# Layer 3 in runs of 3, 8, 7 and 4 row tiles, with the last normalisation folded into weights

## The chip, the core and the metric

The kernel runs on one core of one Trainium2 chip. A core has five engines that run beside each other and meet only at semaphores: TensorE (matrix products, into PSUM), VectorE and ScalarE (element by element), GpSimd (the same, more slowly, and not on PSUM) and SyncE (which issues transfers). The metric is device time in microseconds, the median of several executions. Every engine executes its own instructions strictly in the order in which they were issued; an instruction that waits holds up all that are queued behind it on its engine.

## The reference, cut to what matters

Four graph layers follow one another, each on the normalised output of the one before, with 2708 nodes and 128 features. The change touches only the end of layer 3, an attention layer with two heads:

```python
def _L3_gnn_ref(x, adj, ff0_w, ff1_w, attn_w, g1, b1, g2, b2):   # x is h = relu(layernorm(xs))
    x_norm = _ln(x, g1, b1)
    mask = (adj > 0) | jnp.eye(n, dtype=bool)
    h_next = jnp.zeros((n, co), x.dtype)
    for i in range(2):
        h = x_norm @ ff0_w[i].T
        s_src = h @ attn_w[i, :c]
        s_dst = h @ attn_w[i, c:]
        e = jnp.where(mask, leaky_relu(s_src[:, None] + s_dst[None, :]), NEG)
        att = softmax(e, axis=1) @ h + x
        att = _ln(att, g2, b2)                       # (att - mean) / sqrt(var + eps) * g2 + b2
        h_next = h_next + elu(att @ ff1_w[i].T) / 2
    return h_next
...
h = jnp.maximum(_layernorm(x, axis=-1), 0.0)
x = x + _L3_gnn_ref(h, adj, ...)
```

## The kernel before, in words

The 2708 rows form 22 tiles of 128 rows; the last tile has 20. All of layer 3's inputs stay on the chip: `xs` (the rows so far), `h3` (their normalised, rectified form), `mask` (the transposed adjacency as bytes), `row` and `lift` (factors of the attention weights by destination and by source), and `hv` (128 features and a column of weights for the softmax denominator, per head).

The attention product is done in *runs* of row tiles, `RUNS = ((0, 3), (3, 8), (11, 8), (19, 3))`, each pair being first tile and number of tiles. `products` (L943 to L967) walks through 44 units per run (22 source tiles, two heads). For each unit VectorE first makes the weights of the whole run with one instruction, `weigh` (L930), into a tile `wt`; three units later in the issue order TensorE multiplies each 128-column piece of `wt` with `hv` (L960) and accumulates in PSUM. One product of 128x128 with 129 columns appears as two matmul records and two weight loads in the profile. Three sums of 129 columns share a PSUM bank, so a run of 8 tiles (16 sums) takes six banks and a run of 3 takes two.

Where the run's columns aren't a multiple of 128, as in the last run (276 columns), `weigh` writes into one of five tiles `padded`, which GpSimd sets once (L1238), in turn. Otherwise it takes one of five rotating buffers `wt`.

When a run is done, `evacuate` (L991) copies its banks from PSUM to SBUF, on ScalarE and every third one on VectorE, and `close` (L1012) finishes two row tiles (four sums) at a time: division by the denominator and addition of `h3` (L1023), row statistics and their power -1/2 on GpSimd (`moments`, L118 to L121), a Newton step and the shift (`factors`, L127 to L131), scaling on ScalarE (L137), four transposes on TensorE (L1034), a ScalarE copy that applies `g2` and `b2` (L1037), the second product with `ff1T` (L1043), the ELU in three ScalarE instructions (L1051 to L1053) with sums on GpSimd (L1055 to L1057), and two VectorE instructions (L1060, L1061) before the store to `out` (L1066).

The order on each engine is written out by hand. `close` is a generator; its `yield` gives a distance in ticks of a clock that `products` advances by 0.29 per tile and unit (`spend`), and `close` itself by its own TensorE work. `close_run` (L1068) begins a new pair every `apart` ticks, 9 by default. So the closes of a run are spread between the units of the next run. The last run has no run behind it: its sums are read where they are (`in_place`, L975), its two closes begin 2 ticks apart, and nothing covers them.

A flag, counted on the way (`lost_rows`), is turned into a count on TensorE and VectorE at the very end (L1707, L1708) and read by the engines; with a count over zero the program would go on with `dense_layers`.

Of the kernel before, what the change touches and what calls it, by code (L numbers as in the profile page):

```python
# [20 lines left out]
F32 = mybir.dt.float32  # L21
BF16 = mybir.dt.bfloat16
AF = mybir.ActivationFunctionType
# [7 lines left out]
P = 128  # L31
# [20 lines left out]
def size(t):  # L52
    return min(P, N - t * P)
# [7 lines left out]
def listed_layers(ctx: ExitStack, tc: tile.TileContext, x, adj, w, out, flag):  # L61
# [827 lines left out]
    score = l3.tile([P, NT, 4], F32, name="score")  # L889
    nc.gpsimd.memset(score[:, NT - 1, :], 0.0)  # L890
    nc.gpsimd.memset(hv[:, NT - 1, :, :], 0.0)
    nc.gpsimd.memset(lift[:, NT - 1, :], 0.0)
    nc.gpsimd.memset(mask[:, NT - 1, :], 0)
    ident_8 = l3.tile([P, P], U8, name="ident_8")
    nc.vector.tensor_copy(ident_8, ident)
    PIECE = 5
    RUNS = ((0, 3), (3, 8), (11, 8), (19, 3))
    MOST = 8
    accs = ctx.enter_context(tc.tile_pool(name="l23p", bufs=1, space=PSUM))

# [4 lines left out]
    def follow(steps):  # L905
        following.append([steps, clock[0]])
# [62 lines left out]
    def banks_of(run, numbers):  # L969
# [1 line left out]
            accs.tile([P, CH], F32, tag=f"acc{b}", name="att")[:, 0 : 3 * (D + 1)].rearrange("p (s d) -> p s d", s=3)  # L971
            for b in numbers[0 : (2 * run[1] + 2) // 3]
        ]

    def in_place(run, banks):  # L975

        r0, rn = run
        sums = [banks[s // 3][:, s % 3, :] for s in range(2 * rn)]
        inv3 = out_pool.tile([P, 2 * MOST], F32, name="inv3")
        for k in range(2):  # L980
            for q0, q1 in ((0, rn - 1), (rn - 1, rn)):
                m, s = size(r0 + q1 - 1), k * rn
                if q1 > q0:
                    nc.vector.reciprocal(
                        inv3[0:m, s + q0 : s + q1], banks[s // 3][0:m, (s + q0) % 3 : (s + q1 - 1) % 3 + 1, D]
                    )
        return sums, inv3, False

    def evacuate(run, banks):

        r0, rn = run  # L991
        res = out_pool.tile([P, 2 * MOST, D + 1], F32, bufs=1, name="res")
        inv3 = out_pool.tile([P, 2 * MOST], F32, name="inv3")
        tails = (rn - 1, 2 * rn - 1) if size(r0 + rn - 1) < P else ()
        for s in tails:
            nc.gpsimd.memset(res[:, s, :], 1.0)
        s = 0
        while s < 2 * rn:
            k = min(3 - s % 3, 2 * rn - s)
            m = P  # L1000
            if s in tails:
                k, m = 1, TAIL
            elif s + k - 1 in tails:
                k -= 1
            copy = nc.vector.tensor_copy if s // 3 % 3 == 2 else nc.scalar.copy
            copy(res[0:m, s : s + k, :], banks[s // 3][0:m, s % 3 : s % 3 + k, :])
            s += k
        nc.vector.reciprocal(inv3[:, 0 : 2 * rn], res[:, 0 : 2 * rn, D])
        return [res[:, s, :] for s in range(2 * rn)], inv3, True

    def close(run, sums, first):

        res, inv3, whole = sums
        k0 = min(2, run[1] - first)
        t0 = run[0] + first
        n = 2 * k0
        att = out_pool.tile([P, 4, D], F32, name="att_s")
        for s in range(n):
            i = s % 2 * run[1] + first + s // 2
            m = P if whole else size(t0 + s // 2)  # L1020
            if m < P:
                nc.gpsimd.memset(att[:, s, :], 0.0)
            nc.vector.scalar_tensor_tensor(  # L1023
                att[0:m, s, :], res[i][0:m, 0:D], inv3[0:m, i : i + 1], h3[0:m, t0 + s // 2, :],
                op0=ALU.mult, op1=ALU.add,
            )
        rows = tiles_of(att, 0, n)
        mv = moments(rows, "n4")
        yield 4.5
        scale_rows(rows, rows, *factors(*mv), AF.Identity)  # L1030
        yield 4
        p = bank("p_aT")
        for s in range(n):
            nc.tensor.transpose(p[:, s * P : (s + 1) * P], att[:, s, :], ident)  # L1034
        spend(0.25 * n)
        zT = out_pool.tile([P, 4, P], F32, name="z4T")
        nc.scalar.activation(  # L1037
            zT[:, 0:n, :], p.rearrange("p (s i) -> p s i", s=4)[:, 0:n, :], AF.Identity, bias=shift2, scale=gain2
        )
        yield 1.5  # L1040
        p = bank("p_o")
        for s in range(n):
            nc.tensor.matmul(  # L1043
                p[:, s * D : (s + 1) * D], zT[:, s, :], ff1T[:, s % 2 * D : (s % 2 + 1) * D], start=True, stop=True
            )
        spend(0.33 * n)

        v = p.rearrange("p (q k d) -> p q k d", q=2, k=2)[:, 0:k0, :, :]
        el = out_pool.tile([P, 2, 2, D], F32, name="el")[:, 0:k0, :, :]
        po = out_pool.tile([P, 2, 2, D], F32, name="po")[:, 0:k0, :, :]  # L1050
        nc.scalar.activation(el, v, AF.Relu, scale=-1.0)  # L1051
# [5 lines left out]
        nc.gpsimd.tensor_tensor(less[:, 0:k0, :], less[:, 0:k0, :], po[:, :, 0, :], ALU.add)  # L1057
# [3 lines left out]
        nc.vector.scalar_tensor_tensor(  # L1061
            y[:, 0:k0, :], el[:, :, 0, :], 0.5, less[:, 0:k0, :], op0=ALU.mult, op1=ALU.add
        )
        for q in range(k0):
            m, i = size(t0 + q), (t0 + q) * P
            nc.sync.dma_start(out[i : i + m, :], y[0:m, q, :])  # L1066

    def close_run(run, sums, apart=9):  # L1068
# [164 lines left out]
    nc.vector.reduce_sum(over, wide, AX.XY)  # L1233
    nc.vector.tensor_tensor(flag, flag, over, ALU.add)

    for q in range(5):
        padded.append(out_pool.tile([P, RUNS[-1][1] * P], F32, tag=f"padded{q}", bufs=1, name=f"padded{q}"))
        nc.gpsimd.memset(padded[q], 0.0)  # L1238

    with tc.tile_pool(name="l3w", bufs=5) as wpool, tc.manual_schedule():  # L1240
        for run, numbers in zip(RUNS[1:], ((2, 3, 4, 5, 0, 1), (2, 3, 4, 5, 0, 1), (2, 3))):

            def work_off(last=last, banks=banks):
                follow(close_run(last, evacuate(last, banks)))

            banks = products(run, numbers, wpool, 3, work_off)
            last = run
        follow(close_run(last, in_place(last, banks), 2))
        while following:
            spend(1)  # L1250
            advance()


@with_exitstack
# [459 lines left out]
```

## Time and profile before

| what | us |
|---|---|
| median of 3 runs (lowest, highest) | 1063.11 (1061.25, 1065.79) |
| the profiled execution | 1066.37 |
| its span | 1064.6 |
| run (3,8): first product to the next run | 829.7 to 911.8 |
| run (11,8) | 911.8 to 1000.2 |
| run (19,3) | 1000.2 to 1041.8 |
| last product to the last VectorE instruction | 1041.8 to 1058.6 |
| from there to the end of the span | 6.0 |

Over the whole span TensorE is busy 929.8 us (87%), VectorE 826.0 (78%), ScalarE 515.7 (48%) and GpSimd 402.1 (38%). Such shares are means over stages with different limits, so they say little about an edit at the end of layer 3; for this the span is cut into stretches and the order of instructions is read there.

In the profile PE is TensorE, PEld its weight load, DVE VectorE, ACT ScalarE, POOL GpSimd and SP SyncE. A timeline row gives start, length, engine, line, operation, output and inputs, shapes, and how many like instructions were merged into it; in brackets stands how long the engine had been idle before and what ended that. In a table by stretch each engine has its busy time and, in brackets, its number of instructions; then follow the clock that was granted to TensorE as a share of full speed, and the share and rate of the transfers.

### The profile page before, as it was taken

Reading aid. Unit: us, or ns where it says so; the run is one execution under the profiler, and the core shown is the slowest. Engines: PE = TensorE matmul, PEld = TensorE weight load, DVE = VectorE, ACT = ScalarE, POOL = GpSimd, SP = SyncE. Lnnn points to the kernel's source line nnn. Section 1 sums busy time; section 2 is a strip of 40 time slices with the busy share of each in tenths; the row PEclk is TensorE's granted clock in tenths of the full one; section 3 lists DMA queues with packets and bytes.
Section 4 is the critical chain, followed back from the end, with each engine's and each line's share of the span. In section 5 each row is a group of like instructions: output and inputs, shape, how many; then the busy total and the mean of one; then the engine's idle time right before and its main releaser. Section 6 shows DMA issues by size and latency. Waiting matters only on the chain. (4 is left out here: it accounts for less than half of the span.)

```text
span 1064.6 us, 22002 instructions
## 1 busy us (share of the span) xinstructions
PE 929.8 (87%) x7950; PEld 749.6 (70%) x7950; DVE 826.0 (78%) x2853; ACT 515.7 (48%) x1428; POOL 402.1 (38%) x486
## 2 busy tenths in 40 slices
PE   5788889943799999999999959999989999999983
PEld 2454455432699999899999924444478899989982
DVE  7999999868577798887878264655678987997793
ACT  7787787534766666666666521433322200230142
POOL 3310112022776657666766163344311200250042
PEclk9999999756899999999999979999989999999996
DMA  9888997221233423222231066556410000000000
GB/s 366 305 316 288 320 354 256 77 62 55 77 106 122 125 91 111 100 93 88 91 103 57 28 211 207 196 184 226 124 38 21 8 8 1 2 16 6 1 11 19
DMA packets 60626, 129.67 MB, mean 122 GB/s; under 512 B 11161, under 2 KB 23829, under 8 KB 57799
## 3 DMA queue, kind: packets, MB, share of 16 engines
q1 hardware_dynamic: 58690, 125.38, 34.5%
q10 hardware_dynamic: 1816, 2.80, 1.0%
q8 instruction: 64, 1.05, 0.4%
q14 instruction: 56, 0.45, 0.1%
HBM read 81.55 MB, written 30.87 MB: 106 GB/s over the span
## 5 line engine op out<-in xcount | busy, mean ns | idle before, releaser
L960 PE MATMUL att<-hv,wt 128*128 128x129 f32 x1672 | 194.4, 277 | 8.7 <-DVE wt L930 8.7
L960 PEld LDWEIGHTS att<-hv,wt 128*128 128x128 f32 x1672 | 190.9, 193 | 11.7 <-DVE wt L930 8.6
L539 POOL TENSOR_SCALAR put<-mine,value 128x128 f32<-128x128 bf16 x176 | 149.6, 866 | 69.1 <-DVE mine L436 51.4
L615 PE MATMUL p_m<-s,sel 128*128 128x128 bf16 x1452 | 160.8, 219 | 5.4 <-ACT g L627 5.4
L619 PE MATMUL p_m<-d,cols 124*128 124x128 bf16 (+1 forms) x1452 | 161.2, 219 | 1.3 <-DVE cols L569 1.2
L930 DVE SCALAR_TENSOR_TENSOR wt<-row,lift,mask 128x1024 f32<-128x1024 f32 (+1 forms) x132 | 138.7, 1081 | 23.3 <-PE att L960 23.3
L121 POOL TENSOR_TENSOR n_r<-n_r,minus_half 128x4 f32<-128x4 f32 (+1 forms) x31 | 46.3, 1492 | 270.8 <-DVE n_r L120 265.2
L640 PE MATMUL agg<-put,g 128*128 128x128 f32 (+1 forms) x968 | 135.9, 281 | 0.0
L297 PE MATMUL acc<-a,hs 128*128 128x512 f32 (+2 forms) x264 | 124.5, 574 | 11.2 <-ACT hs L137 11.2
L1099 PE MATMUL p_agg<-a,hs 128*128 128x512 f32 (+2 forms) x264 | 110.5, 561 | 13.0 <-DMA a<-adjT 12.9
L309 PEld LDWEIGHTS p_T<-ident,a 128*128 128x128 f32 x484 | 59.6, 143 | 88.3 <-issue 40.1
L640 PEld LDWEIGHTS agg<-put,g 128*128 128x128 f32 x968 | 118.2, 192 | 0.0
L615 PEld LDWEIGHTS <-sel 128*128 128x128 bf16 x1452 | 104.7, 98 | 9.7 <-issue 7.1
L285 DVE FIND_INDEX8 col<-val,a 128x8 uint16<-128x124 f32 (+1 forms) x400 | 104.8, 269 | 0.0
L309 PE MATMUL p_T<-ident,a 128*128 128x128 f32 x484 | 81.8, 287 | 26.2 <-ACT aT L313 20.0
L619 PEld LDWEIGHTS <-cols 124*128 124x128 bf16 (+1 forms) x1452 | 102.0, 97 | 1.9 <-DVE cols L569 1.9
L627 ACT ACTIVATE g<-p_m 128x512 f32<-128x512 f32 x132 | 73.0, 553 | 61.6 <-PE p_m L619 61.6
L547 ACT ACTIVATE put<-mine,value 128x128 f32<-128x128 bf16 x308 | 100.5, 391 | 0.0
L313 ACT ACTIVATE aT<-p_T 128x512 f32<-128x512 f32 (+2 forms) x132 | 71.1, 541 | 46.9 <-ACT aT L313 31.4
L283 DVE MAX8 val<-a 128x8 f32<-128x124 f32 (+1 forms) x400 | 90.1, 261 | 1.9 <-DMA a<-in_adj 1.9
L1099 PEld LDWEIGHTS p_agg<-a,hs 128*128 128x128 f32 (+1 forms) x264 | 47.8, 195 | 61.9 <-issue 53.0
L297 PEld LDWEIGHTS acc<-a,hs 128*128 128x128 f32 (+1 forms) x264 | 44.7, 202 | 26.7 <-issue 15.3
(260 smaller groups left out, 1504.4 us busy)
## 6 DMA issues: line engine op xcount, KB each, us to landing
a<-in_adj SPq DMA_DIRECT2D x21, 1354.0 KB
adjT<-aT SPq DMA_DIRECT2D x105, 256.0 KB
a<-adjT SPq DMA_DIRECT2D x20, 1280.0 KB
spread<-passed SPq DMA_DIRECT2D x22, 704.0 KB
later<-sel SPq DMA_DIRECT2D x22, 616.0 KB
row<-own_d ACTq DMA_DIRECT2D x10, 256.0 KB
later<-sel SPq DMA_DIRECT2D x22, 82.5 KB
adjT<-aT SPq DMA_DIRECT2D x21, 74.0 KB
```

Source lines behind the costliest of these rows:

```text
L283: nc.vector.max(val[:, n, b, :], block(b))
L285: nc.vector.max_index(col[:, n, b, :], val[:, n, b, :], block(b))
L297: nc.tensor.matmul(accs[ci][:, 0:cw], h[0:m, n, :], sets[n // 4][0:m, n % 4, c : c + cw], start=(n == 0), stop=(n == NT - 1),)
L309: nc.tensor.transpose(p[0:k, q * P : q * P + m], sets[gi][0:m, q, j * P : j * P + k], ident[0:m, 0:m])
L539: nc.gpsimd.tensor_scalar(st["put", 0][:, b, :], st["mine"][:, b, :], st["value"][:, b : b + 1], None, ALU.mult)
L547: nc.scalar.activation(st["put", 1][:, b - HP, :], st["mine"][:, b, :], AF.Identity, scale=st["value"][:, b : b + 1])
L615: nc.tensor.matmul(p[:, b - b0, :], st["sel"][:, b, :], s3[:, q, t % 2, :], start=(q == 0), stop=False)
L619: nc.tensor.matmul(p[:, b - b0, :], st["cols"][0:kb, b, :], d3[0:kb, b, q, :], start=False, stop=(q == 2))
L640: nc.tensor.matmul(agg, g[:, b - 4 * k, :], put, start=(b == 0), stop=False)
L930: nc.vector.scalar_tensor_tensor(wt[:, 0:n], row[:, k, c : c + n], lift[:, j, k : k + 1], mask[:, j, c : c + n], op0=ALU.max, op1=ALU.mult,)
L960: nc.tensor.matmul(banks[s // 3][:, s % 3, :], wt[:, q * P : (q + 1) * P], hv[:, j, k, :], start=(v < 2 and s // 3 not in touched), stop=( ...
L1099: nc.tensor.matmul(pa[:, 0:n], h[0:k, j, :], a[0:k, j - j0, 0:n], start=(j == 0), stop=(j == NT - 1))
```

## The change

The runs become (0,3), (3,8), (11,7) and (18,4). The last run's four tiles (404 columns of weights, eight sums, three banks) are closed by a new function `close_last`, all at once. It rests on this: with the mean and the gain moved into the weights, `(layernorm(a) * g2 + b2) @ W` is `rstd * (a @ folded) + offset`, where `folded` is `g2 * W` less its column means and `offset` is `b2 @ W`. So the unnormalised `a` can be transposed and multiplied before its statistics are known, and the product's rows are scaled by `rstd` afterwards, on VectorE. `fold_weights` makes `folded`, `offset` (halved, as the ELU's mean over two heads asks) and `less` (`xs - 1`, in place) ahead of run (3,8). `rstd` carries the other half (constants -0.25 and 0.75 of the Newton step), and the exponential takes a scale of 2.

The run (11,7) is evacuated and closed during the last run as before, but with its closes 6 ticks apart. `padded` has four tiles of 512 columns, set to 1.0, instead of five of 384. `h3`'s last tile is set to zero, so that rows past the end hold numbers. `in_place` goes.

```diff
+    nc.gpsimd.memset(h3[:, NT - 1, :], 0.0)
...
-    RUNS = ((0, 3), (3, 8), (11, 8), (19, 3))
+    RUNS = ((0, 3), (3, 8), (11, 7), (18, 4))
...
+    def fold_weights():
+
+        both = out_pool.tile([P, 2, D], F32, tag="y", name="both")
+        even, flat = both[:, 0, :], both[:, 1, :]
+        nc.gpsimd.memset(even, 1.0 / D)
+        nc.gpsimd.tensor_scalar(flat, even, shift2, float(D), ALU.mult, ALU.mult)
+        folded = out_pool.tile([P, 2 * D], F32, bufs=1, name="folded")
+        nc.gpsimd.tensor_scalar(folded, ff1T, gain2, None, ALU.mult)
+        p = bank("p_even")
+        nc.tensor.matmul(p[:, 0 : 2 * D], even, folded, start=True, stop=True)
+        nc.tensor.matmul(p[:, 2 * D : 4 * D], flat, ff1T, start=True, stop=True)
+        nc.vector.tensor_tensor(folded, folded, p[:, 0 : 2 * D], ALU.subtract)
+        offset = out_pool.tile([P, 2, D], F32, bufs=1, name="offset")
+        nc.scalar.activation(offset, p[:, 2 * D : 4 * D].rearrange("p (k d) -> p k d", k=2), AF.Copy, scale=0.5)
+        t0, rn = RUNS[-1]
+        less = xs[:, t0 : t0 + rn, :]
+        nc.gpsimd.tensor_scalar(less, less, -1.0, None, ALU.add)
+        return folded, offset, less
+
+    def close_last(run, banks):
...
+        for b in range(0, ns, 3):
+            k = min(3, ns - b)
+            nc.vector.reciprocal(inv3[:, b : b + k], banks[b // 3][:, 0:k, D])
+        room = out_pool.tile([P, 2 * MOST, D + 1], F32, tag="res", bufs=1, name="room")
+        att, zT = room[:, 0:ns, 0:D], room[:, ns : 2 * ns, 0:D]
+        v = att.rearrange("p (q k) d -> p q k d", k=2)
...
+        for q0, q1 in parts:
+            p = bank("p_aT")
+            for q in range(q0, q1):
+                for k in range(2):
+                    s, i = 2 * q + k, k * rn + q
+                    nc.vector.scalar_tensor_tensor(
+                        att[:, s, :], banks[i // 3][:, i % 3, 0:D], inv3[:, i : i + 1], h3[:, t0 + q, :],
+                        op0=ALU.mult, op1=ALU.add,
+                    )
+                    nc.tensor.transpose(p[:, (s - 2 * q0) * P : (s - 2 * q0 + 1) * P], att[:, s, :], ident)
+            n = 2 * (q1 - q0)
+            nc.scalar.copy(zT[:, 2 * q0 : 2 * q1, :], p[:, 0 : n * P].rearrange("p (s i) -> p s i", s=n))
+        for s in range(ns):
+            nc.vector.bn_stats(st[:, s, :], att[:, s, :])
+        for s in range(ns):
+            nc.vector.bn_aggr(mv[:, s, :], st[:, s, :])
+        rstd, ve, tmp = (r[:, i, :] for i in range(3))
+        nc.vector.tensor_scalar(ve, mv[:, :, 1], EPS, None, ALU.add)
+        nc.gpsimd.tensor_tensor(rstd, ve, minus_half[:, 0:ns], ALU.pow)
+        nc.vector.tensor_tensor(tmp, rstd, rstd, ALU.mult)
+        nc.vector.tensor_tensor(tmp, tmp, ve, ALU.mult)
+        nc.vector.tensor_scalar(tmp, tmp, -0.25, 0.75, ALU.mult, ALU.add)
+        nc.vector.tensor_tensor(rstd, rstd, tmp, ALU.mult)
+        lows = []
+        for q0, q1 in parts:
+            p = bank("p_o")
+            for s in range(2 * q0, 2 * q1):
+                nc.tensor.matmul(
+                    p[:, (s - 2 * q0) * D : (s - 2 * q0 + 1) * D], zT[:, s, :],
+                    folded[:, s % 2 * D : (s % 2 + 1) * D], start=True, stop=True,
+                )
+            for s in range(2 * q0, 2 * q1):
+                nc.vector.scalar_tensor_tensor(
+                    v[:, s // 2, s % 2, :], p[:, (s - 2 * q0) * D : (s - 2 * q0 + 1) * D], rstd[:, s : s + 1],
+                    offset[:, s % 2, :], op0=ALU.mult, op1=ALU.add,
+                )
+            low = out_pool.tile([P, 2, 2, D], F32, tag="el", name="low")[:, 0 : q1 - q0, :, :]
+            nc.vector.tensor_scalar(low, v[:, q0:q1, :, :], 0.0, None, ALU.min)
+            nc.scalar.activation(low, low, AF.Exp, scale=2.0)
+            for k in range(2):
+                nc.vector.scalar_tensor_tensor(
+                    less[:, q0:q1, :], v[:, q0:q1, k, :], 0.0, less[:, q0:q1, :], op0=ALU.max, op1=ALU.add
+                )
+            lows.append(low)
+        for (q0, q1), low in zip(parts, lows):
+            y = out_pool.tile([P, 2, D], F32, name="y")
+            nc.vector.tensor_tensor(low[:, :, 0, :], low[:, :, 0, :], low[:, :, 1, :], ALU.add)
+            nc.vector.scalar_tensor_tensor(
+                y[:, 0 : q1 - q0, :], low[:, :, 0, :], 0.5, less[:, q0:q1, :], op0=ALU.mult, op1=ALU.add
+            )
+            for q in range(q0, q1):
+                m, i = size(t0 + q), (t0 + q) * P
+                nc.sync.dma_start(out[i : i + m, :], y[0:m, q - q0, :])
...
-    for q in range(5):
+    for q in range(4):
         padded.append(out_pool.tile([P, RUNS[-1][1] * P], F32, tag=f"padded{q}", bufs=1, name=f"padded{q}"))
-        nc.gpsimd.memset(padded[q], 0.0)
+        nc.gpsimd.memset(padded[q], 1.0)
 
     with tc.tile_pool(name="l3w", bufs=5) as wpool, tc.manual_schedule():
-        for run, numbers in zip(RUNS[1:], ((2, 3, 4, 5, 0, 1), (2, 3, 4, 5, 0, 1), (2, 3))):
+        folds = fold_weights()
+        for run, numbers in zip(RUNS[1:], ((2, 3, 4, 5, 0, 1), (2, 3, 4, 5, 0), (1, 2, 3))):
 
             def work_off(last=last, banks=banks):
-                follow(close_run(last, evacuate(last, banks)))
+                follow(close_run(last, evacuate(last, banks), 9 if run != RUNS[-1] else 6))
 
             banks = products(run, numbers, wpool, 3, work_off)
             last = run
-        follow(close_run(last, in_place(last, banks), 2))
         while following:
             spend(1)
             advance()
+        close_last(last, banks)
```

More of the change, by code (lines that the diff above doesn't have):

```diff
@@ L973, in banks_of @@
         ]
[L975 to L987, printed above, removed]
     def evacuate(run, banks):
@@ new lines, in close_last @@
+    def close_last(run, banks):
+        t0, rn = run
+        ns = 2 * rn
+        folded, offset, less = folds
+        inv3 = out_pool.tile([P, 2 * MOST], F32, name="inv3")
+        for b in range(0, ns, 3):
[4 more added lines that the diff above has]
+        v = att.rearrange("p (q k) d -> p q k d", k=2)
+        st = out_pool.tile([P, ns, 6], F32, bufs=1, name="st_l")
+        mv = out_pool.tile([P, ns, 2], F32, bufs=1, name="mv_l")
+        r = out_pool.tile([P, 3, ns], F32, bufs=1, name="r_l")
+        parts = [(q, min(q + 2, rn)) for q in range(0, rn, 2)]
+        pT = []
+        for q0, q1 in parts:
[51 more added lines that the diff above has]
+                nc.sync.dma_start(out[i : i + m, :], y[0:m, q - q0, :])
```

## The prediction

> **What bounds the kernel now.** I read the page first, then busy time by window, the waits, and the order of instructions at the two places that the change touches. The change lies in layer 3, the last 240 us. Busy time by stretch there (columns: length, then busy us and instructions of TensorE, its weight load, VectorE, ScalarE, GpSimd, then granted clock and DMA):
> ```profile
> 828.00:829.70 1.70, 0.27 (x3) 0.08 (x1) 1.42 (x2) 0.56 (x2) 0.00 (x0) 1.00 0.12 15
> 829.70:911.80 82.10, 81.40 (x722) 80.67 (x723) 67.33 (x83) 7.88 (x17) 10.31 (x8) 1.00 0.02 5
> 911.80:1000.20 88.40, 85.74 (x755) 84.22 (x754) 73.63 (x128) 18.04 (x36) 21.31 (x16) 1.00 0.03 7
> 1000.20:1041.80 41.60, 37.10 (x314) 35.40 (x312) 36.70 (x122) 16.59 (x33) 14.83 (x16) 1.00 0.04 11
> 1041.80:1058.60 16.80, 5.52 (x20) 3.82 (x20) 8.75 (x39) 6.00 (x14) 5.88 (x11) 0.69 0.04 12
> 1058.60:1064.60 6.00, 0.00 (x0) 0.00 (x0) 0.00 (x0) 0.00 (x0) 0.00 (x0) 0.50 0.12 29
> ```
> The second and third rows are the runs (3,8) and (11,8): TensorE is busy 99% and 97%. The fourth is the run (19,3): TensorE and VectorE are both near 89%, and each waits for the other. The fifth is the tail after the last product: no engine is full, a dependent chain passes between them. The waits from 829 us to 1042 us (total us, times, longest) say the same:
> ```profile
> DVE wt L930 <- PE att L960: 23.3, 45, 1.4
> PEld att L960 <- DVE padded L930: 6.0, 8, 1.3
> PE att L960 <- DVE padded L930: 4.5, 7, 1.1
> ```
> In the long runs VectorE waits for TensorE; in the last one TensorE waits for `padded`. The tail in order of time, cut to its joints:
> ```profile
> 1041.82 0.22 DVE L984 RECIPROCAL inv<-att 128x2 f32<-128x2 f32 x2 [0.45 <-PE att L960]
> 1041.97 1.09 DVE L1023 SCALAR_TENSOR_TENSOR att_s<-att,inv,h 128x128 f32<-128x128 f32 x4
> ...
> 1044.95 1.14 POOL L121 TENSOR_TENSOR n_r<-n_r,minus_half 128x4 f32<-128x4 f32 x1 [3.11 <-DVE n_r L120]
> ...
> 1048.81 2.42 ACT L137 ACTIVATE att_s<-att_s,n_r 128x128 f32<-128x128 f32 x6 [8.07 <-DVE n_r L131]
> ...
> 1051.95 2.93 PE L1043 MATMUL p_o<-ff1T,z4T 128*128 128x128 f32 x12 [0.19 <-ACT z4T L1037]
> 1054.06 0.60 ACT L1051 ACTIVATE el<-p_o 128x512 f32<-128x512 f32 x1 [1.70 <-PE p_o L1043]
> ...
> 1058.30 0.29 DVE L1061 SCALAR_TENSOR_TENSOR y<-el,less 128x128 f32<-128x128 f32 x1 [0.41 <-POOL less L1057]
> ```
> Statistics, power, scaling, transposes, product and ELU follow one another. Fold and scaling by row take the two ScalarE passes and the transposes off this chain.
>
> **Units.** In the full stretch 960 to 980 us TensorE does 181 records in 20 us; a run of 8 paces one `wt` each 1.787 us, so a tile costs 1.787/8 = 0.223 us per unit, 9.83 us per run of 44 units. `weigh` takes 0.43 us for 276 columns in a row of them and 1.20 for 1024; on the straight line between, 0.57 for 404 and 1.07 for 896. A close of two tiles costs VectorE 1.05 (four L1023) + 1.6 + 0.2 (statistics) + 1.0 (L127 to L131) + 0.87 (L1060, L1061) = 4.7 us, and TensorE 0.44 + 0.89 = 1.33.
>
> **1. Run (11,8) becomes (11,7).** Before: 44 x 1.787 + 4 x 1.33 = 84.0 us of TensorE in 88.4, so 4.4 idle, at the two places where transposes wait for ScalarE behind late factors (939.2 and 949.8 us). After: 44 x 1.564 + 5.3 = 74.1. Walking the changed order by hand, each close still brings 8.3 us of VectorE per 7 us of TensorE, and three units of lead are now 4.7 us instead of 5.4; idle grows to 5.4 (bounds 3 and 8). 79.5, or -8.9 us.
>
> **2. Run (19,3) becomes (18,4).** Before: 44 x 0.670 + 5.3 = 34.8 of TensorE in 41.6, 6.8 idle. After: 44 x 0.893 + 4.7 (seven tiles closed) = 44.0. The closes begin 6 ticks apart instead of 9, and the tick counts 1.16 per unit, so they stand closer. Walked with four `padded` buffers (unit u waits for the product u-4): VectorE leads until about 30 us into the run, with TensorE idle 1 us after each of the first three bursts of statistics and 0.8 us at one group of transposes: 4.1 us. Then it is 18 units of pure TensorE work. GpSimd in the same stretch lengthens VectorE work: L130 takes 0.65 instead of 0.16 us beside L1056, a `wt` 1.76 instead of 1.24 beside L1057. I add 0.4 per close, 1.5. Total 49.6, or +8.0 (bounds: no idle but the first 1 us, +3.4; the old idle plus 2 us, +11). The start gains nothing: bank 1 is free, but TensorE did not wait there before (products run through 1000.2 us). Parts 1 and 2 together: -0.9.
>
> **3. The fold, ahead of run (3,8).** Its VectorE subtraction stands in front of the first `wt`, which stands in front of the first product; behind it queue all later weighs. Before, the first `wt` waits for the last product of run (0,3) and TensorE for the `wt`:
> ```profile
> 828.28 4.87 DVE L930 SCALAR_TENSOR_TENSOR wt<-row,lift,mask 128x1024 f32<-128x1024 f32 x4 [1.44 <-PE att L960]
> 829.62 10.99 PE L960 MATMUL att<-hv,wt 128*128 128x129 f32 x96 [1.43 <-DVE wt L930]
> ```
> After, two 256-column products come first (a `p_hv` product of 260 columns takes 0.60 us, less when others follow closely), then the subtraction (a 256-column PSUM operation near 0.45), then the `wt`. TensorE's own part and the second product lie beside that. +0.9 us (bounds 0.5 and 1.6). ScalarE's `offset` delays its evacuation of banks 0 and 1 by some 2 us; they are needed 2.7 us into the run, so nothing. The row DMAs queued behind it serve columns first used in the last run. GpSimd's inputs are done about 804 us, 24 us early. The memset of `h3` and four of `padded` for five (0.42 us each at 384 columns) fall where GpSimd has nothing else to do.
>
> Those GpSimd instructions (two TENSOR_SCALARs between 801 and 804 us, one of 512 columns after 806) run beside run (0,3), where VectorE is busy 23.4 of 28 us. Beside the TENSOR_SCALAR L1055, L127 and L129 grew by 0.27 us together (927.2 us), so +0.3 (bounds 0 and 0.8). SBUF — State Buffer of the Trainium skill, section Who interferes with whom, says that a GpSimd instruction that reads SBUF and a VectorE one with two SBUF inputs block each other for the whole instruction. By it the three would cost up to their own 4 us, with 1.8 taken from the 512-column L1094; the rows show that full block for GpSimd's two-input L1056 only.
>
> **4. The tail.** On VectorE, from the last product: one reciprocal left, 0.25; eight L1023-like at 0.26 (1.09 for four), 2.1; eight statistics, 1.8, by this row (two at 0.22 apart):
> ```profile
> 4.05 0.48 DVE L118 BATCH_NORM_STATS2 n_st<-xs 128x6 f32<-128x128 f32 x2 [3.04 <-DMA xs<-in_x]
> ```
> then eight aggregates at 0.10, 0.9, and the EPS add 0.2: 5.3 us. Transposes, ScalarE copies and the products of the folded weights are done beside that. GpSimd's power over 8 columns lies between 1.14 (4 columns) and this one:
> ```profile
> L228 POOL TENSOR_TENSOR flat<-flat,minus_half 128x18 f32<-128x18 f32 x1 | 3.3, 3252 | 0.1
> ```
> I take 1.8, with 0.2 around it: 7.3. Four Newton steps 0.8. Each half: four scale-and-offset 1.05, `low` 0.45, two maxima 0.9; two halves 4.8, with the flag's cast between them up to 0.6 more. The exponentials hide there. Both `y` pairs 1.8. That is 15.0 us, against 16.8. The last two stores now leave together and one is 64 KB where it was 10: +0.5. Part 4: -1.3 (bounds -3, if the power takes 1.14 and statistics 0.18; +1.0, if each instruction costs its full duration without overlap, 16.7 us, and the cast's wait 0.6 comes on top).
>
> **Sum:** -0.9 + 0.9 + 0.3 - 1.3 = -1.0 us. The profiled execution took 1066.37 us (span 1064.6), 3.3 above the median 1063.11; it would become 1065.4, and the median 1062.1. 0.5% (5.3 us) is what a measurement of this kernel can tell from no change, so this is no change.
>
> **Rivals.** (a) *The last run becomes TensorE's.* For it: a unit gives TensorE 0.89 us against 0.57 of VectorE, where it was 0.67 against 0.43, and one tile fewer is closed. Then only about 1 us of idle stays in part 2 and the tail reaches its low end: -4.6 - 1.7 on top, 1055.8. Against it: the waits before show that a burst of 2.85 us empties three units, and those are 2.7 us.
> (b) *Slower: the clock at the fold.* The granted clock halves after a gap elsewhere:
> ```profile
> 782.97 2.92 PE L960 MATMUL att<-hv,wt 128*128 128x129 f32 x12 [2.74 <-DVE wt L930]
> ...
> 784.00:786.00 2.00, 2.00 (x11) 2.00 (x11) 0.41 (x1) 0.00 (x0) 0.00 (x0) 0.50 0.03 8
> ```
> About 7 us at half speed follow, 3.5 us lost. It decides if the gap in front of run (3,8) comes near 2.74 us; I expect 1.4, as now, with the clock at 1.00. Price +3.5, 1065.6. TensorE: Matmul & The Clock Gate of the Trainium skill, section HAM oscillation, warns of idle gaps over some 3.4 us; by it neither gap would halve the clock, and the first one did.
> (c) *Slower: the tail does not overlap.* 39 VectorE instructions become 51 and ScalarE's share moves to VectorE. At full durations it is the 17.3 us of part 4's upper bound, +2.3 on the sum: 1064.4. From a tail of 16.0 us on the change costs time.
> (d) *The fold buys nothing:* the power, not the scaling, ends the wait, tail as before: 1063.4.
>
> **Numbers.** Forecast 0.55, (a) 0.17, (b) 0.08, (c) 0.10, (d) 0.10. The forecast's own range is 1059.5 to 1064.5; to leave out 2 in 10 I go down to 1057.0, into (a), and up to 1066.5, past (b) and (c). Faster by over 0.5% (below 1057.8): most of (a) and a little of the forecast, 0.17. Slower (above 1068.4): only the ends of (b) and (c) and what I do not see, 0.08. The rest, 0.75, is no change.
>
> **What would show it.** First product of run (3,8) at 0.9 us later against the end of run (0,3), clock 1.00; run (11,7) near 79.5 us; run (18,4) near 49.6 with TensorE waiting 3 to 6 us for `padded`; power 1.8 us; last product to last `y` near 15.0 us. The prediction is wrong if the last run's idle vanishes or doubles, if eight statistics in a row cost 0.4 us each, or if a layer before the fold moves.

## The result, and the profile after

The changed kernel takes 1063.70 us (median of 12 executions, 1061.22 to 1066.84), the kernel before 1064.66 us (12 executions beside them, 1061.25 to 1067.79). The ratio is 0.9998, with a 95% interval from 0.9987 to 1.0009: no change, as forecast. The profiled execution took 1062.77 us with a span of 1061.0 us.

A ratio of one does not say that nothing happened. I cut both traces at the same five events: the end of the last product of run (0,3), the first product of each following run, the end of the last product, the end of VectorE's last `y`, the end of the span. All lengths below are us.

| stretch | before | after | difference |
|---|---|---|---|
| end of run (0,3) to first product of run (3,8) | 1.43 | 2.62 | +1.19 |
| run (3,8) | 82.26 | 82.21 | -0.05 |
| run (11,8), after (11,7) | 88.35 | 79.46 | -8.89 |
| run (19,3), after (18,4) | 41.56 | 50.07 | +8.51 |
| last product to last `y` | 16.81 | 13.49 | -3.32 |
| last `y` to the end of the span | 5.99 | 8.04 | +2.05 |
| sum | 236.39 | 235.88 | -0.51 |

Up to there the two profiled executions differ by 3.1 us, about as much as executions of one kernel do, so everything below is read from the end of run (0,3) on. The stretches of the changed kernel, with busy us and instructions of TensorE, its weight load, VectorE, ScalarE and GpSimd, then granted clock and transfers:

```profile
825.10:827.70 2.60, 0.85 (x4) 0.42 (x4) 1.71 (x3) 1.14 (x3) 0.00 (x0) 1.00 0.01 3
827.70:909.90 82.20, 81.54 (x722) 80.79 (x723) 67.03 (x83) 7.88 (x18) 10.29 (x8) 1.00 0.02 5
909.90:989.40 79.50, 77.73 (x667) 76.06 (x666) 68.53 (x128) 17.83 (x36) 19.14 (x16) 0.98 0.03 8
989.40:1039.45 50.05, 45.98 (x396) 44.28 (x394) 42.65 (x117) 14.69 (x32) 14.79 (x16) 1.00 0.04 10
1039.45:1052.95 13.50, 4.05 (x26) 3.06 (x26) 11.26 (x49) 2.43 (x4) 1.67 (x1) 0.83 0.01 2
1052.95:1061.00 8.05, 0.00 (x0) 0.00 (x0) 0.00 (x0) 0.00 (x0) 0.00 (x0) 0.50 0.14 36
```

In the fifth row VectorE is now busy 11.26 of 13.5 us, where it was 8.75 of 16.8: the chain between engines has become VectorE's own list. The last row is longer by 2.05 us, three fifths of the 3.32 that the row above it gained. The waits between 829 and 1045 us (total us, times, longest) show the last run's idle, in four to five waits where there were seven to eight, and longer ones:

```profile
PEld att L961 <- DVE padded L931: 5.0, 5, 1.8
PE att L961 <- DVE padded L931: 4.0, 4, 1.6
```

The place of the fold in the timeline of the changed kernel:

```profile
824.93 0.60 PE L1064 MATMUL p_even<-folded,both 128*128 128x256 f32 x2
825.36 0.59 PE L1065 MATMUL p_even<-ff1T,both 128*128 128x256 f32 x2
825.99 0.42 DVE L1066 TENSOR_TENSOR folded<-folded,p_even 128x256 f32<-128x256 f32 x1 [2.25 <-PE p_even L1065]
826.33 4.87 DVE L931 SCALAR_TENSOR_TENSOR wt<-row,lift,mask 128x1024 f32<-128x1024 f32 x4
```

VectorE's subtraction reads only what L1064 wrote, but it started when L1065, the second product into the same bank, was done (825.95). Then come the four weighs, and TensorE's first product behind the first of them. The tail, cut to its joints:

```profile
1039.57 2.14 DVE L1096 SCALAR_TENSOR_TENSOR room<-att,inv,h 128x128 f32<-128x128 f32 x8
1041.63 1.64 DVE L1104 BATCH_NORM_STATS2 st_l<-room 128x6 f32<-128x128 f32 x8
1043.18 0.62 DVE L1106 BATCH_NORM_AGGREGATE mv_l<-st_l 128x2 f32<-128x6 f32 x8
1044.09 1.67 POOL L1109 TENSOR_TENSOR r_l<-r_l,minus_half 128x8 f32<-128x8 f32 x1 [16.79 <-DVE r_l L1108]
1046.67 1.13 DVE L1123 SCALAR_TENSOR_TENSOR room<-p_o,r_l,offset 128x128 f32<-128x128 f32 x4
1052.17 3.36 SPq L1143 DMA_DIRECT2D out<-y  x4
1052.51 0.42 DVE L1138 SCALAR_TENSOR_TENSOR y<-low,xs 128x256 f32<-128x256 f32 x1
```

Statistics cost 0.20 each and aggregates 0.08, the power over eight columns 1.67. The row of the stores spans 3.36 us: SyncE's four issues stand one behind the other. By the trace they take 0.33, 0.82, 1.11 and 0.91 us and the last one ends at 1055.53, 2.6 us after the last `y`; the span ends 5.5 us after that. Before, the issues were three:

```profile
1057.38 1.54 SPq L1066 DMA_DIRECT2D out<-y  x3
```

The last of them took 0.31 us, ended 0.3 us after `y`, and the span ended 5.7 us after it.

### The profile page after: what moved, and what is told of

Its sections match the earlier page's. It is cut to its first block, busy times and chain, and to the rows that moved or that the text cites. A ratio compares the mean times of both kernels' runs of the same rounds, so it can differ in the third digit from the quotient of the medians.

```text
span 1061.0 us, 21996 instructions
## 1 busy us (share of the span) xinstructions
PE 929.2 (88%) x7954; PEld 751.0 (71%) x7954; DVE 829.3 (78%) x2859; ACT 510.2 (48%) x1417; POOL 399.6 (38%) x481
## 5 line engine op out<-in xcount | busy, mean ns | idle before, releaser
L961 PE MATMUL att<-hv,wt 128*128 128x129 f32 x1584 | 185.0, 277 | 9.1 <-DVE wt L931 7.3
L961 PEld LDWEIGHTS att<-hv,wt 128*128 128x128 f32 x1584 | 181.5, 193 | 12.2 <-DVE wt L931 6.9
L931 DVE SCALAR_TENSOR_TENSOR wt<-row,lift,mask 128x384 f32<-128x384 f32 (+2 forms) x132 | 132.3, 1036 | 19.7 <-PE att L961 19.7
L121 POOL TENSOR_TENSOR n_r<-n_r,minus_half 128x4 f32<-128x4 f32 (+1 forms) x29 | 44.0, 1519 | 248.8 <-DVE n_r L120 244.8
L285 DVE FIND_INDEX8 col<-val,a 128x8 uint16<-128x124 f32 (+1 forms) x400 | 108.1, 285 | 0.0
L283 DVE MAX8 val<-a 128x8 f32<-128x124 f32 (+1 forms) x400 | 92.7, 275 | 2.6 <-DMA a<-in_adj 2.6
```

The lines of the kernel that those rows point to most:

```text
L283: nc.vector.max(val[:, n, b, :], block(b))
L285: nc.vector.max_index(col[:, n, b, :], val[:, n, b, :], block(b))
L931: nc.vector.scalar_tensor_tensor(wt[:, 0:n], row[:, k, c : c + n], lift[:, j, k : k + 1], mask[:, j, c : c + n], op0=ALU.max, op1=ALU.mult,)
L961: nc.tensor.matmul(banks[s // 3][:, s % 3, :], wt[:, q * P : (q + 1) * P], hv[:, j, k, :], start=(v < 2 and s // 3 not in touched), stop=( ...
```

## The experiments

The question is not why the time changed but what cancelled. My theory: the change has two halves of opposite sign, a fold that gains and a redistribution of tiles that gives it back, and both ends of the fold (its insertion, its stores) leak part of the gain. The table holds all the runs, in us by the stretches above; "front" is the stretch in front of run (3,8), "runs" the sum of the three runs behind it, "tail" the stretch from the last product to the last `y`, and "stores" the one from there to the end of the span. Ratios are to the kernel before on the same chip. The stretches are those of one profiled execution each, so the ratios, which hold several, need not agree with them to a microsecond.

| kernel | front | runs | tail | stores | sum | ratio (95%) |
|---|---|---|---|---|---|---|
| before | 1.43 | 212.17 | 16.81 | 5.99 | 236.39 | |
| changed | 2.62 | 211.74 | 13.49 | 8.04 | 235.88 | 0.9998 (0.9987 to 1.0009) |
| 1 fold, old runs | 2.62 | 212.15 | 11.54 | 8.26 | 234.57 | 0.9956 (0.9942 to 0.9969) |
| 1 again | 2.62 | 212.17 | 11.53 | 7.14 | 233.46 | 0.9972 (0.9959 to 0.9985) |
| 2 new runs, no fold | 1.43 | 213.24 | 19.37 | 6.99 | 241.03 | 1.0031 (1.0020 to 1.0042) |
| 3 closes 9 apart | 2.62 | 210.45 | 13.49 | 7.30 | 233.86 | 0.9976 (0.9960 to 0.9992) |
| 4 stores on two queues | 2.62 | 213.27 | 13.49 | 6.69 | 236.07 | 0.9983 (0.9971 to 0.9996) |
| 5 fold behind four weighs | 1.43 | 213.43 | 13.50 | 7.80 | 236.17 | 0.9998 (0.9985 to 1.0011) |
| 6 longer gap | 3.28 | 211.73 | 13.48 | 7.92 | 236.41 | 1.0010 (0.9994 to 1.0025) |
| 7 1 + 4 + 5 | 1.43 | 213.88 | 11.55 | 6.00 | 232.86 | 0.9967 (0.9956 to 0.9977) |
| 9 fold behind the evacuation | 1.43 | 212.08 | 13.47 | 7.89 | 234.87 | 0.9977 (0.9960 to 0.9994) |
| 10 1 + 4 + 9 | 1.43 | 214.14 | 11.54 | 6.85 | 233.96 | 0.9962 (0.9949 to 0.9976) |
| 11 as 10, power by pair | 1.43 | 214.13 | 11.64 | 6.17 | 233.37 | 0.9954 (0.9940 to 0.9967) |

### 1. The fold with the old runs

```diff
-    RUNS = ((0, 3), (3, 8), (11, 7), (18, 4))
+    RUNS = ((0, 3), (3, 8), (11, 8), (19, 3))
-    for q in range(4):
+    for q in range(5):
-        for run, numbers in zip(RUNS[1:], ((2, 3, 4, 5, 0, 1), (2, 3, 4, 5, 0), (1, 2, 3))):
+        for run, numbers in zip(RUNS[1:], ((2, 3, 4, 5, 0, 1), (2, 3, 4, 5, 0, 1), (2, 3))):
-                follow(close_run(last, evacuate(last, banks), 9 if run != RUNS[-1] else 6))
+                follow(close_run(last, evacuate(last, banks)))
```

> Fold and folded tail, with the runs of the kernel before (3, 8, 8, 3; closes 9 apart; five padded buffers). Theory A, the two parts of the change have opposite signs: the fold gains, the new runs give it back. The stretch in front of run (3,8) stays 2.8 us (as in the changed kernel), run (11,8) 88.4 and run (19,3) 41.6 as before; the tail has six sums: 4.66 - 1.10 for two fewer of STT, statistics and aggregates, power 1.4 (between 1.14 for 4 columns and 1.67 for 8), Newton 0.9, first half 2.4, second 1.4, y 1.3 = about 11.1 us against 16.8 before; last y to the end 7.2 against 6.0. Sum 1.3 - 5.7 + 1.2 = -3.2 us against the kernel before, ratio 0.997. Theory B, fold and runs need each other (the tail's gain comes from four whole tiles that are worked together): tail near 15.5, sum +1 us, ratio 1.001.

Measured: 1058.93 us against 1063.58, and measured again (number 8, below) 1059.54 against 1063.11. The tail is 11.54 us, close to theory A's 11.1 and far from B's 15.5. Tail and end in the table by stretch:

```profile
1040.60:1052.15 11.55, 3.30 (x21) 2.37 (x20) 9.52 (x43) 1.94 (x4) 1.46 (x2) 0.87 0.05 13
1052.15:1060.40 8.25, 0.00 (x0) 0.00 (x0) 0.00 (x0) 0.00 (x0) 0.00 (x0) 0.50 0.12 28
```

Theory A holds: the fold alone shortens the tail by 5.3 us, pays 1.2 in front and 1.2 to 2.3 at the stores. It does not need four tiles.

### 2. The new runs without the fold

```diff
-        folds = fold_weights()
-        close_last(last, banks)
+        follow(close_run(last, in_place(last, banks), 2))
```

The cut is shown against the changed kernel. `in_place` is that of the kernel before, its reciprocals cut at the bank boundaries, which a run of four tiles crosses; `padded` is preset to 0.

> New runs (3, 8, 7, 4; closes of the last run 6 apart; four padded buffers) without the fold: the last run is closed as before, by statistics, scaling and transposes of two pairs of tiles. Theory A: run (11,7) 79.5, run (18,4) 50.0, in front of run (3,8) 1.4 us; the tail now closes four tiles where it closed three, so 16.8 + 2 to 3 us, about 19.3; last y to the end 6.3. Sum -0.5 + 2.5 + 0.3 = +2.3 us, ratio 1.002. Theory B (my prediction's parts 1 and 2 taken as the whole price of the runs, with a tail that takes four tiles as it took three): -0.9 us, ratio 0.999.

Measured: 1066.98 us against 1063.58, slower by 0.2 to 0.42%. The tail is 19.37 us, as theory A had it. Two rows of that tail's timeline say what the fourth tile costs:

```profile
1046.78 3.19 ACT L137 ACTIVATE att_s<-att_s,n_r 128x128 f32<-128x128 f32 x8 [21.02 <-DVE n_r L131]
1050.68 3.78 PE L1045 MATMUL p_o<-ff1T,z4T 128*128 128x128 f32 x16 [0.19 <-ACT z4T L1039]
```

Eight row scalings take 3.19 us where six took 2.42, sixteen records of products 3.78 where twelve took 2.93. Moving a tile from run (11,8) to the last run is nearly neutral inside the runs and costs 2.6 us behind them. Of the +1.07 in the runs, 1.5 us is a half-clock stretch in run (11,7), told under "not expected".

Together the two experiments add up: about -3.0 to -4.7 us for the fold and +3.3 for the runs, where both together measured -0.2 us.

### 3. The closes of the last run 9 apart

```diff
-                follow(close_run(last, evacuate(last, banks), 9 if run != RUNS[-1] else 6))
+                follow(close_run(last, evacuate(last, banks), 9))
```

> The changed kernel with the closes in the last run 9 ticks apart as in the other runs, not 6. Theory A (my walk: idle of TensorE comes from each burst of statistics that outlasts the units in padded, four bursts whatever their distance): run (18,4) 50.0 within 0.7, TensorE's wait for padded 4 to 5 us as now, and less pure product work behind the last close. Rival: with more room between bursts VectorE regains its lead, and the run drops by 2 us or more, to 48.

Run (18,4) took 48.78 us instead of 50.07, which it took within 0.03 us in all six traces with closes 6 apart: a gain below the rival's 2 us and above my 0.7. The waits between 989 and 1037.8 us:

```profile
PEld att L961 <- DVE padded L931: 4.2, 6, 1.4
PE att L961 <- DVE padded L931: 3.0, 5, 1.2
```

Both kinds fall, PE's from 4.0 to 3.0 us, in shorter pieces. The distance between closes is a knob worth about a microsecond, which the change gave away; my walk had the idle depend only on the bursts.

### 4. The last stores on two queues

```diff
-                nc.sync.dma_start(out[i : i + m, :], y[0:m, q - q0, :])
+                (nc.scalar if q % 2 else nc.sync).dma_start(out[i : i + m, :], y[0:m, q - q0, :])
```

> The changed kernel with the last four stores alternating between SP's and ScalarE's queue. Theory A (the four issues stand in one line on SP, 0.33, 0.86, 1.1, 0.9 us each, the last one ending 2.6 us after y): with two in each line the last issue ends 0.9 to 1.3 us after the last y, and the end of the span comes 6.3 to 6.6 us after the last y, against 8.07: -1.5 us. Rival: the wait is not the queue but the data (a 64 KB transfer's landing at 5.5 us after its issue, two at once share the DMA engines): the end stays 8 us after the last y.

Last `y` to the end: 6.69 us instead of 8.04, just above theory A's 6.3 to 6.6, and not the rival's 8. The issues run side by side:

```profile
1052.69 1.98 SPq L1143 DMA_DIRECT2D out<-y  x2
1052.69 2.01 ACTq L1143 DMA_DIRECT2D out<-y  x2
```

The last one ends 1.25 us after `y` instead of 2.6, and the span 5.4 us after that, about as in the changed kernel (5.5). So the line on the queue is the cause and not the landing. The size of the gain is less sure than this pair of traces says, for the four issues on one queue vary: the five traces of the changed tail on one queue (changed kernel, numbers 3, 5, 6 and 9) took 7.30 to 8.04 us here, so two queues save 0.6 to 1.35. (Its run (11,7) took 81.00 us, for a half-clock stretch as in the second experiment; the whole shows little of the gain in the profile's sum.)

### 5. The fold behind the first four weighs

```diff
-        folds = fold_weights()
+        folds = []
             def work_off(last=last, banks=banks):
+                if not folds:
+                    folds.extend(fold_weights())
```

> The changed kernel with the fold emitted behind the first four weighs of run (3,8) instead of ahead of them. Theory A (the 1.2 us that the fold adds in front of run (3,8) are the two products and the subtraction standing in VectorE's queue before the first weigh): the gap from run (0,3)'s last product to the first product of run (3,8) falls from 2.62 to 1.43 us, as in the kernel before; the two products lie in that gap, and the subtraction, 0.42 us on VectorE, delays the fifth weigh, for which TensorE does not wait; run (3,8) stays 82.2 to 82.3. Rival: the products of the fold lie on TensorE's own path, and 0.9 us of the 1.2 stay in the gap.

The gap fell to 1.43 us as theory A said, and the time did not move: run (3,8) grew from 82.21 to 83.94.

```profile
830.00 0.41 DVE L1066 TENSOR_TENSOR folded<-folded,p_even 128x256 f32<-128x256 f32 x1
830.49 0.38 ACT L1068 ACTIVATE offset<-p_even 128x256 f32<-128x256 f32 x1 [9.11 <-DVE folded L1066]
831.30 4.96 PE L961 MATMUL att<-hv,wt 128*128 128x129 f32 x42 [1.81 <-ACT res L993]
```

A wait took the place of the one removed. ScalarE's `offset` stood behind the subtraction until 830.49, the copies out of run (0,3)'s banks (L993) stood behind `offset`, and TensorE, which came to need bank 0 after 24 records, 2.95 us into the run, waited 1.81 us for them. Neither theory had it.

### 9. The fold behind the evacuation too

```diff
             def work_off(last=last, banks=banks):
+                sums = evacuate(last, banks)
+                if not folds:
+                    folds.extend(fold_weights())
-                follow(close_run(last, evacuate(last, banks), 9 if run != RUNS[-1] else 6))
+                follow(close_run(last, sums, 9 if run != RUNS[-1] else 6))
```

> The changed kernel with the fold emitted behind the first four weighs and also behind the evacuation of run (0,3)'s banks. Theory A (the wait of 1.81 us that took the place of the shortened gap is TensorE waiting for ScalarE's copy out of a bank, which stood behind the fold's offset on ScalarE, which stood behind VectorE's subtraction): with the copies ahead of the offset the gap stays 1.43 us and run (3,8) comes back from 83.94 to 82.3; 1.2 us in all against the changed kernel. Rival (the copies are late because VectorE's four weighs stand ahead of something that they need, or the fold's two products cost TensorE's path their time): run (3,8) stays 83 or more.

Gap 1.43, run (3,8) 82.59: theory A, short of 0.3 us. ScalarE's copies now come first:

```profile
828.24 1.11 ACT L993 COPY res<-att 128x387 f32<-128x387 f32 x2 [3.14 <-PE att L961]
```

The wait of 1.81 us is gone. What remains is a stop between two products at 839.2 us, whose records start 0.30 us apart instead of 0.11. The trace puts it on VectorE: the weight load at 839.49 stood idle for 0.22 us until a weigh was done. The subtraction now stands in VectorE's list ahead of the fifth weigh, which began 3.9 us into the run, where it was 3.5 in the changed kernel. So TensorE does in the end wait for some of the delay that my expectation in number 5 called free.

### 6. A longer gap in front of run (3,8)

```diff
+        for _ in range(2):
+            spare = out_pool.tile([P, 2, D], F32, tag="y", name="spare")
+            nc.vector.tensor_copy(spare, p[:, 0 : 2 * D].rearrange("p (k d) -> p k d", k=2))
```

> The changed kernel with two idle copies (256 columns, out of the fold's own bank, 0.4 us each) added on VectorE behind the subtraction, so that TensorE stands about 0.9 us longer in front of run (3,8): 2.6 to 2.7 us of idle instead of 1.76. Theory A (my rival (b), that a gap near 2.74 us halves the granted clock, as in front of run (0,3)): run (3,8) grows from 82.2 by 1.7 to 3.5 us, with a half clock in its first 4 to 7 us. Theory B (the half clock in run (0,3) comes from what stands ahead of it, not from the one gap): gap +0.9, run (3,8) 82.2, clock 1.00.

The copies cost 0.33 us each, the gap grew by 0.66 and not the intended 0.9, to 3.28 us, of which TensorE stood idle 2.42:

```profile
827.30:909.55 82.25, 81.58 (x723) 80.84 (x724) 67.07 (x83) 7.96 (x19) 10.28 (x8) 1.00 0.02 6
```

Run (3,8) took the same 82.2 us at a clock of 1.00. Theory B: an idle of 2.42 us here does not halve the clock, so my rival (b) was priced from a place that does not carry over. The idle stayed below the 2.74 us in front of run (0,3); whether those would have done it here was not tried.

### 7, 8, 10 and 11. Towards a better version

Number 7 joins numbers 1, 4 and 5.

> Fold and folded tail with the runs of the kernel before (as in the first experiment), the fold behind the first four weighs, and the last stores alternating between SP's and ScalarE's queue. If the parts add up, against that first experiment: -1.2 us in front of run (3,8), -1.3 us of stores; from the end of run (0,3) 234.6 - 2.5 = 232.1 us, against 236.4 before and 235.9 for the changed kernel: ratio to before 0.996 by the profile's stretches (0.993 if the first experiment's median is taken for the base). Rival (the end is bound by the transfers, and the saved wait returns elsewhere): 234 us or more, ratio 0.998.

Number 8 is number 1 again, on the same chip beside number 7 ("1 again" in the table).

> The kernel of the first experiment once more, beside the one above on the same chip. Its ratio there, 0.9956 (4.7 us), was more than the 1.8 us that its profiled execution shows from the end of run (0,3) on. Theory A (execution scatter ahead of the change, five runs): ratio 0.997 to 0.9985. Theory B (the kernel also gains ahead of run (0,3), or its profiled execution was no typical one): 0.9956 again, and the place shows in the start of run (0,3) or in the stores at the end.

Number 8 gave 0.9972 (0.9959 to 0.9985), in theory A's range. But the two profiled executions of this kernel differ by 1.1 us in the stores (8.26 and 7.14), the place that theory B named, so the scatter is not all ahead of the change. The profiles' -1.8 and -2.9 us and the two ratios are compatible near -3. Number 7 gave 232.86 us by stretches and 0.9967: stores 6.00 as hoped, but the fold's gain is lost as in number 5. Number 10 takes number 9's place for the fold instead.

> The runs of the kernel before, fold behind four weighs and behind the evacuation, last stores on two queues. If the parts add up: gap 1.43, run (3,8) 82.3, (11,8) 88.4, (19,3) 41.6, tail 11.5, stores 6.0: 231.2 us from the end of run (0,3), 5.2 less than before and 1.7 less than with the fold ahead of the evacuation; ratio 0.995 to 0.996. Rival: the 1.7 us do not come back, ratio 0.997.

Run (3,8) fell to 82.59, but run (11,8) took 89.98 us where number 7 took 88.35, for reasons of the clock told below, and the stores 6.85 instead of 6.00, so the sum is 233.96 and not the 231.2 expected; the ratio is 0.9962 (0.9949 to 0.9976), 1059.45 against 1063.89 us. Number 11 splits statistics and power by pair:

```diff
+            half = slice(2 * q0, 2 * q1)
+            nc.vector.tensor_scalar(ve[:, half], mv[:, half, 1], EPS, None, ALU.add)
+            nc.gpsimd.tensor_tensor(rstd[:, half], ve[:, half], minus_half[:, 0:n], ALU.pow)
```

with the four Newton steps per pair too.

> As the kernel above, but the last run's two pairs (four and two sums) each have statistics, aggregates and a power of their own, so that GpSimd's first power lies beside VectorE's work on the second pair. Theory A (VectorE's wait of 1.5 to 1.7 us for the one power is idle that other work can fill; four small Newton steps and one add come on top, 1.0 us): tail 10.6 to 10.9 us against 11.5. Rival (GpSimd's two-input power lengthens VectorE's instructions beside it, as L1056 lengthened L130 from 0.16 to 0.65 us): tail 11.5 or more.

The tail took 11.64 us, as the rival had it, but not for the rival's reason. The wait for the power is gone, and VectorE's small instructions beside the power took 0.15 to 0.19 us, as alone. TensorE now does the second pair's transposes ahead of the first pair's products, and VectorE waits for these:

```profile
1045.73 1.13 DVE L1124 SCALAR_TENSOR_TENSOR room<-p_o,r_l,offset 128x128 f32<-128x128 f32 x4 [0.60 <-PE p_o L1119]
```

That 0.6 us and the doubled small instructions use up what was won. The order of TensorE's work is only a part of the 0.6 us. In this trace a half-clock stretch begins at 1043.94 us, and the records of the products (L1119) start 0.21 us apart, against 0.11 in number 10. At 0.11 the first pair's eight records, begun at 1043.86, would have been done near 1044.9, ahead of VectorE's Newton steps, which ended at 1045.13. By this estimate from the rows some 0.5 us of the tail is the clock's; no run shows this tail without the stretch. Its ratio, 0.9954 (0.9940 to 0.9967), cannot be told from number 10's. Both beat the kernel before by 0.4 to 0.5%, and the changed kernel, with its ratio of 0.9998, by about as much. Most of it is the fold kept and the redistribution left out, for number 1 has 0.9956 and 0.9972 with that alone; what the late fold and the two queues add on the old runs, the ratios cannot tell.

## Why the prediction was right, and where its steps were not

The forecast was no change, -1.0 us; the traces say -0.51 from the end of run (0,3) on, and the ratio -0.2 ± 1.2 us. The mechanism was right in the main: the gain lies behind the last product, the fold costs time in front of run (3,8), and the new runs leave TensorE waiting for `padded`. By its terms:

- **Runs, -0.9.** Measured -0.38 (-8.89 and +8.51). Run (11,7) was 79.46 (forecast 79.5) and run (18,4) 50.07 (49.6), with TensorE waiting 4 to 5 us for `padded` (3 to 6). The counts of units times pace carried this; the walk's idle, set by the bursts whatever their distance, was wrong by 1.3 us (number 3). Some luck lies in the 79.46: with a half-clock stretch 10 us later in the run, the same run took 80.92 and 81.00 in numbers 2 and 4. What parts 1 and 2 call idle before, 4.4 and 6.8 us, is what counts times pace leave; by the busy times in the prediction's own rows TensorE was idle 2.7 and 4.5 us. And 1 us after each of three bursts plus 0.8 make 3.8, not 4.1.
- **Fold, +0.9.** Measured +1.19. The step that failed is "TensorE's own part and the second product lie beside that": the subtraction waited for both products of its bank, 0.43 us more than for the first alone. Number 5 shows that the whole of it comes from standing ahead of the first weigh.
- **`offset` costs nothing.** Right where it was put (826.50, copies right behind), and number 5 shows the cover going: 4 us later, the same instruction cost 1.81 us.
- **GpSimd beside run (0,3), +0.3.** Mis-sized: nothing. That run took 45.22 us in the kernel before, and 45.17 to 45.19 in numbers 1, 3, 4 and 6, all with a half-clock stretch of 6.8 us at its start; with one of 3.4 us it took 44.10 without the fold (number 2) and 44.11 and 43.98 with it (changed kernel, number 8). The block for the whole instruction, of which the Trainium skill, SBUF — State Buffer, tells in the sections SBUF: two separate sides and Who interferes with whom, does not show in these lengths.
- **Tail compute, 16.8 to 15.0.** Measured 13.49. Power 1.67 (1.8) was right. Mis-sized were what stands ahead of it, 4.6 us instead of 5.3 (statistics 0.20 each and not 0.22, aggregates 0.08 and not 0.10, nothing lost between them), the two halves with the cast between, 4.7 us instead of 5.1, and the power with the waits around it, 1.8 instead of 2.0.
- **Stores, +0.5.** Measured +2.05 (+1.3 to +2.05 over the five traces of this tail on one queue). I counted the larger transfer and forgot the queue: four issues in one line on SyncE, 3.36 us, and not 0.3 to 0.4 each as in the rows before. The two errors of part 4 cancel almost exactly: -1.27 against the forecast -1.3. That is luck, and a reader should not take the matching sum for a matching account.

Two sums of the prediction are off without touching its forecast: part 4's lower bound, with a power of 1.14 and statistics of 0.18, gives about -2.3 and not -3, which moves rival (a) from 1055.8 to 1056.5, and rival (d), a tail as before with the stores' +0.5 kept, gives 1063.9 and not 1063.4.

Of the rivals, (a) fell because the waits for `padded` stayed, (b) by the clock of 1.00 with a gap of 2.62 and even of 3.28 us (and its reading was off: the half clock of the kernel before began at 781.84 us, 1.6 us into the gap of 2.74, and not after it), (c) because the tail overlapped better than forecast, (d) because the tail shrank by 3.3 us. What the prediction did not say, though its terms held it, is that the fold is worth 5.3 us of tail on three tiles and 5.9 on four, and that the fourth tile costs 2.0 to 2.6: the sign of the change was decided by the moved tile, not by the fold.

## What to carry to other kernels

When a change bundles a gain with a rearrangement, price each half against the kernel before on its own; two halves of 3 us that cancel look like "nothing happened", and here the better kernel was one of the halves. Work moved off a critical gap is only moved: list what is queued behind it at its new place on every engine that it touches, as the `offset` that delayed the bank copies shows. At the end of a kernel count the issues of the last stores on each queue as a chain of their own, and leave few row tiles behind the last product (here the fourth cost 2.0 to 2.6 us; fewer than three were not tried).

## What the runs showed of the hardware that I had not expected

- **The issues of the last stores vary in length.** On SyncE the last stores took 0.33 us for the first issue and 0.3 to 1.7 for the following, in no fixed order (0.82, 1.11, 0.91 in the changed kernel; 1.71, 0.43, 0.36 in number 9), while pairs earlier in layer 3 took 0.33 and 0.42. What lengthens one and not another the runs do not show. From the end of the last issue the span went on for 5.2 to 6.0 us in all kernels.
- **A half-clock stretch costs by where it falls.** In run (11,7) or (11,8) most of the traces have one of 3.4 us, about where transposes waited for ScalarE. Near 937 to 943 us (changed kernel, numbers 1, 3, 7, 8, 9) the run is no longer than without one; in number 7 the next transposes, which came later, no longer had to wait. Near 947 to 948 us (numbers 2, 4, 10, 11) the run is 1.5 to 1.6 us longer. In number 10 the records are:

```profile
946.36 1.48 PE L1021 MATMUL p_aT<-ident,att_s 128*128 128x128 f32 x4 [1.06 <-ACT att_s L137]
947.68 3.02 PE L961 MATMUL att<-hv,wt 128*128 128x129 f32 x16
```

  Sixteen records take 3.02 us there and 1.95 at full clock. The single waits ahead of these stretches, where I read them, were only 1.1 to 1.4 us, less than the 2.42 us that did not halve it in number 6, so the length of one gap does not decide. In every trace the stretches begin on a grid of 3.41 us, so it also matters where on the grid a wait falls, which number 6 did not control. Nor does the busy share of one grid window decide: TensorE was busy 1.47 us of the window from 778.42 us in the kernel before, and a half clock followed; in number 6 it was busy 1.49 us of the window from 825.40, and none did. What decides stays open. The Trainium skill, TensorE: Matmul & The Clock Gate, section What's actually happening, tells of a free-running window of 3413 ns over which activity is judged; the lengths of 3.4, 6.8 and 10.2 us in these traces and the grid agree with it. The gap that its section HAM oscillation warns of, over some 3.4 us, was not there ahead of the stretches in the runs of layer 3; the longest was 2.74 us.
- **A reader of a PSUM bank waited for a second writer to another part of it** (0.43 us between L1064's and L1065's end); whether the hardware or only the program's semaphores asked for this, no run shows.
- **GpSimd's power grows with the columns, and beside a weigh.** In the tails it took 0.69 us for 2 columns, 1.04 to 1.14 for 4, 1.35 for 6 and 1.67 for 8. Beside VectorE's weighs in run (3,8) of the changed kernel it took 1.66 for 2 and 1.97 for 4.
